# Moving the axis changes of queries, keys and tokens from TensorE to SBUF-to-SBUF DMAs with VectorE block transposes, and projecting in pairs

## The chip, the core and the metric

The kernel runs on one core of a Trainium2 chip. A core has five engines, each with its own in-order instruction stream: TensorE (PE, matrix products, with weight loads PEld that overlap them), VectorE (DVE), ScalarE (ACT), GpSimd (POOL) and SyncE (SP, which here only issues DMAs). They share an SBUF of 128 partitions. Matrix products go to PSUM. Engines wait for one another, and for DMAs, through semaphores. An instruction that waits holds up everything behind it on its engine.

The metric is the time of one execution on the device, in microseconds (us). Before the change it is 772.0 us, the median of three runs (771.88 to 772.14).

## What is computed

The input `x` is 16 sequences ("batches" below) of 512 tokens with 128 features, all float32. One layer adds to `x` an attention branch and a branch of experts, both fed by a layer norm of `x`:

```
xn = layernorm(x)
# attention: 16 heads of 8 features
q, k, v = xn@Wq, xn@Wk, xn@Wv
q = q / |q| ;  k = k / |k|                       # per head
attn = softmax(causal(8.0 * q @ k.T))
a = (attn @ v) @ Wo
# 8 experts, each token goes to its best 2
p = softmax(xn @ Wr.T); top 2, weights scaled to sum 1
f = sum over the 2 experts of w_e * (gelu(xn @ W1[e].T + b1[e]) @ W2[e].T + b2[e])
return x + a + f
```

The products contract over features, so features must lie on the partitions. The layer norm and the per-head norms leave tokens on the partitions. Something has to change the axes for the normalised tokens (`rows` to `xnT`), for the normalised queries (`qkn` to `qT`) and for the normalised keys (`qkn` to `kr`).

## The kernel before

**Stages.** The attention work is a pipeline of 160 hand-ordered stages, ten for each batch (`PER = 10`), stage `t = 10*b + n`. PE, DVE, ACT and SP keep the order in which the program is written (`manual_schedule`, L924); POOL keeps the order given by `on_pool` (L491). A stage computes score products for batch `b` (`scores`, L655: PE fills two `sim` tiles, ACT takes exponentials of them into `ex`), then a step from the list `side`, then the causal mask of the stage before (`mask`, L682, on DVE when `n` is 1, 4, 6 or 9 and the routing steps are over, otherwise on POOL), then the weighted sum of values of two stages before (`weigh`, L701, PE into the one PSUM bank `av`; after every second or third call DVE transposes `av` into `mid`), and last the steps that `at_stage` planned for this stage (`due`, L1082).

**Preparation of a batch.** `prep(b)` (L551) plans, relative to the batch's first stage: four projections (`proj`, L557, one 128x384 product each, copied out of PSUM by ACT) at -18, -17, -14 and -11; squares on POOL (`squares`, -11 to -9); copies of the values into `vaug` on POOL (`values`); sums of squares and three Newton steps for the inverse root on DVE (`sums`, `root_start`, `root_step`, -7 to -5); the scaling `scale` (L607, DVE) at -4; four PE transposes of queries into a PSUM bank with a DVE copy to `qT` (`turn_q`, L616) at -3; the same for keys into `kr` (`turn_k`, L623) at -2; then four DVE products that keep one head of four each, `kT` (`alone`, L630), at -2, -1, 0 and 1. The batch's first `scores` needs `qT` and the first `kT`.

**Tokens.** Batches 0 to 2 are turned before stage 0. The list `side` (L1029) turns one of batches 3 to 15 in a stage (`turn_x`, L274: four PE transposes, one DVE copy to `xnT`), mixed with the router's logits. Routing steps follow on DVE from stage 20. From then on POOL sends each token's row to two places in DRAM (`send`, L509, 128 indirect DMAs, one or two a stage).

**Experts.** After stage 139 the 71 blocks of the experts run (`experts`, L861), each with four DMAs issued by SP (`fetch`, L776) five blocks ahead. The preparation steps of batch 15 are run inside them, one planned stage every five blocks (L876). The stages of batches 14 and 15 follow.

**Queues.** SP issues the 16 loads of `x`, then 48 DMAs that fill the DRAM table `slots` (L970), and then nothing until the experts. Tiles named from the pool `p1` exist once, those from `p2` twice: a writer waits until all readers of the tile's last use are done. `qkn` and `kr` are single, `qkv` and `qT` are double, and two `vaug` tiles are taken in turn.

Of the kernel before, what the change touches and what calls it, by code (L numbers as in the profile page):

```python
# [10 lines left out]
F32 = mybir.dt.float32  # L11
# [6 lines left out]
HEADS = 16  # L18
# [6 lines left out]
def attention_moe_kernel(  # L25
# [31 lines left out]
    GB = 4  # L57
# [27 lines left out]
    wall = const.tile([P, NQKV], F32, name="wall")  # L85
# [62 lines left out]
    xnT = [xnT2[b // 2][:, b % 2] for b in range(B)]  # L148
# [10 lines left out]
    p1 = pool("p1", 1)  # L159
    p2 = pool("p2", 2)  # L160
# [10 lines left out]
    def misc(name):  # L171
        return ps_m.tile([P, 512], F32, tag="misc", name=name)

    def SIM(name):
# [1 line left out]


    vaugs = [
        p1.tile([P, NC, HEADS, VW], F32, tag=f"vaug{n}", name=f"vaug{n}") for n in range(2)
    ]  # L180


# [91 lines left out]
    def turn_x(b, bank, copy):  # L274

        for c in range(NC):
            nc.tensor.transpose(bank[:, ts(c, P)], rows[b][:, c, :D], ident)
        copy(xnT[b], bank)  # L278


    turned = {}

    def logits(b0):

        lt = misc(f"lt{b0}")
# [205 lines left out]
    def on_pool(op, *args, sent=False, **kw):  # L491

        with ExitStack() as order:
            if issued[0] is not None:
                order.enter_context(tc.issue_after(issued[0].ins))
            if not sent:
                for dma in issued[1]:  # L500
                    order.enter_context(tc.issue_after(dma.ins))
            ins = op(*args, **kw)  # L502
        if sent:
            issued[1].append(ins)
        else:
            issued[:] = [ins, []]
        return ins
# [40 lines left out]
    def at_stage(t, step):  # L548
        plan.setdefault(t, []).append(step)

    def prep(b):  # L551

        t0 = PER * b
        s = live[b] = {}
        s["vaug"] = vaugs[b % 2]

        def proj(c, bank=misc):  # L557
            if not c:
                s["qkv"] = p2.tile([P, NC, NQKV], F32, tag="qkv", name=f"qkv{b}")
            pp = bank(f"proj{b}_{c}")  # L560
            nc.tensor.matmul(  # L561
                pp[:, :NQKV], xnT[b][:, ts(c, P)], wall, start=True, stop=True
            )
            nc.scalar.copy(s["qkv"][:, c], pp[:, :NQKV])  # L564

        heads = lambda t: t.rearrange("p c (h d) -> p c h d", d=DH)
# [7 lines left out]
        def values(c):  # L574
            on_pool(
                nc.gpsimd.tensor_copy,
                s["vaug"][:, c : c + 2, :, 0:DH],
                heads(s["qkv"][:, c : c + 2, 2 * D : 3 * D]),
            )

        n = NC * 2 * HEADS

        def sums():
            s["ss"] = sm.tile([P, n], F32, tag="ss", name=f"ss{b}", bufs=1)
            nc.vector.tensor_reduce(
                s["ss"].rearrange("p (c h) -> p c h", c=NC), heads(s["qkn"]), AX.X, ALU.add
            )

        def root_now(meanwhile):

            s["rn"] = sm.tile([P, n], F32, tag="rn", name=f"rn{b}", bufs=1)
            nc.vector.tensor_scalar_max(s["ss"], s["ss"], L2_EPS * L2_EPS)
            nc.scalar.activation(s["ss"], s["ss"], AF.Sqrt)
            meanwhile()
            nc.vector.reciprocal(s["rn"], s["ss"])

        def root_start():

            s["rn"] = sm.tile([P, n], F32, tag="rn", name=f"rn{b}", bufs=1)
            nc.vector.tensor_scalar_max(s["ss"], s["ss"], L2_EPS * L2_EPS)  # L600
            guess(s["rn"], s["ss"])

        def root_step():
            t = sm.tile([P, n], F32, tag="t", name=f"t{b}")
            newton(s["rn"], s["ss"], t, 1)

        def scale():  # L607
            nc.vector.tensor_mul(
                heads(s["qkn"]),
                heads(s["qkv"][:, :, : 2 * D]),  # L610
                s["rn"].rearrange("p (c h) -> p c h", c=NC).unsqueeze(3).to_broadcast(
                    [P, NC, 2 * HEADS, DH]
                ),
            )

        def turn_q():  # L616
            pt = misc(f"qt{b}")
            for c in range(NC):
                nc.tensor.transpose(pt[:, ts(c, P)], s["qkn"][:, c, :D], ident)  # L619
            s["qT"] = p2.tile([P, S], F32, tag="qT", name=f"qT{b}")  # L620
            nc.vector.tensor_copy(s["qT"], pt)

        def turn_k(bank=misc):  # L623
            pt = bank(f"kt{b}")
            for c in range(NC):
                nc.tensor.transpose(pt[:, ts(c, P)], s["qkn"][:, c, D:], ident)  # L626
            s["kr"] = p1.tile([P, S], F32, tag="turned", name=f"kr{b}")
            nc.vector.tensor_copy(s["kr"], pt)

        def alone(r):  # L630

            if not r:
                s["kT"] = p2.tile([P, NG, S], F32, tag="kT", name=f"kT{b}")
            nc.vector.tensor_scalar_mul(s["kT"][:, r], s["kr"], hmask[:, r : r + 1])  # L634

        if not b:
            return SimpleNamespace(
                proj=proj, squares=squares, values=values, sums=sums, root_now=root_now,
                scale=scale, turn_q=turn_q, turn_k=turn_k, alone=alone,
            )  # L640
        times = (-18, -17, -14, -11) if b > 1 else (-11, -11, -10, -9)
        for c, t in enumerate(times):
            at_stage(t0 + t, lambda c=c: proj(c, SIM if t0 + t < 0 and c else misc))
        for t, step in (
            (-11, lambda: squares(0)), (-11, lambda: squares(1)),
            (-10 + (b == 1), lambda: squares(2)), (-9 + (b == 1), lambda: squares(3)),
            (-8, lambda: values(0)),
            (-7, lambda: values(2)), (-7, sums), (-7, root_start), (-7, root_step),
            (-6, root_step), (-5, root_step), (-4, scale), (-3, turn_q), (-2, turn_k),
            (-2, lambda: alone(0)), (-1, lambda: alone(1)), (0, lambda: alone(2)),  # L650
            (b != B - 1, lambda: alone(3)),
        ):
            at_stage(t0 + t, step)

    def scores(b, n):  # L655
# [328 lines left out]
    for b in range(1, 4):  # L984
        stats(b)
    variance, shifts = scales(1, 4, True)
    for c in range(NC):
        zero.proj(c, SIM if c else misc)
        zero.squares(c)
        if c == 1:  # L990
            variance()
            stats(4)
            shifts()
# [1 line left out]
    normalise(1, (ACT,) * NC)  # L995
    stats(5)
    stats(6)
    zero.values(0)
    zero.values(2)
    normalise(3, (POOL,) * NC)  # L1000
    zero.sums()
    zero.root_now(lambda: stats(7))
# [20 lines left out]

    def turn(b):
        turn_x(b, misc(f"xnt{b}"), nc.vector.tensor_copy)

    side = [  # L1029
        lambda step=step, b=b: step(b)  # L1030
        for step, b in (
            (turn, 3), (turn, 4), (turn, 5), (turn, 6), (turn, 7), (logits, 0),
            (turn_logits, 0), (logits, 4), (turn_logits, 4), (turn, 8), (turn, 9),
            (turn, 10), (turn, 11), (logits, 8), (turn_logits, 8), (turn, 12), (turn, 13),
            (turn, 14), (turn, 15), (logits, 12), (turn_logits, 12),
        )
    ]
# [7 lines left out]
    for t, steps in enumerate(feed):  # L1045
        for step in steps:
            at_stage(t, step)

    (places, later) = place()

# [12 lines left out]
    def stage(t, b, n):  # L1063

        due_masks = masks[:]
        del masks[:]
        if b is not None:
            for _ in range(2 if t % PER in (1, 5, 8) else 1):
                if sends:
                    sends.pop(0)()  # L1070
            if (b, n) != (FIRST, 0):
                scores(b, n)
                pending.append((b, n))
        if side:
            side.pop(0)()
# [84 lines left out]
```

## Time and profile before

The profile is of one execution. That execution took 773.95 us, and its span (first to last instruction) is 772.2 us. The median of the timed runs is 772.0 us, so 1.95 us have to be taken off a sum made against the profiled execution.

| part | us from the span's start | PE busy | DVE busy | ACT busy | POOL busy |
|---|---|---|---|---|---|
| whole span | 0 to 772.2 | 731.1 | 516.6 | 464.8 | 485.9 |
| loads, batch 0 prepared | 0 to 20 | 13.5 | 13.4 | 6.7 | 9.6 |
| first stages | 40 to 70 | 29.0 | 21.4 | 21.9 | 21.3 |
| routing | 150 to 200 | 45.5 | 40.9 | 32.8 | 40.5 |
| attention, later batches | 250 to 300 | 50.0 | 40.6 | 39.7 | 43.6 |
| experts | 440 to 660 | 218.5 | 111.1 | 90.6 | 113.9 |

A row says how long an engine executed instructions in that stretch; what a stretch is limited by is the engine that has no idle time left or, where none is full, the chain of waits. The batches' first stages, read from the `sim` products in the timeline of PE, start at 61.4 (batch 1), 95.8 (2), 122.8 (3), 155.3 (4), 188.9 (5), 217.5 (6), 246.1 (7), then every 26.5 us to 405.1 (13). The experts start at 431.6.

### The profile page before, as it was taken

What the parts mean: (1) busy time and instruction counts of PE and PEld (TensorE: products, weight loads), DVE (VectorE), ACT (ScalarE), POOL (GpSimd) and SP (SyncE); (2) the same over time, 40 slices, a digit from 0 to 9 for tenths busy, and PEclk for the clock granted to TensorE, in tenths of its full rate; (3) what the DMA queues carried; (4) which work ended last, traced back from release to release, by engine and by line L of the source; (5) the groups of instructions that cost most, each with busy time, mean ns of one, the idle gap of its engine ahead of it and who ended that gap; (6) DMA issues with size and microseconds to landing.
All of it is one profiled execution on the core that took longest, in us unless ns stands there. A gap on an engine that the chain in (4) does not pass through costs nothing.

```text
span 772.2 us, 17655 instructions
## 1 busy us (share of the span) xinstructions
PE 731.1 (95%) x6478; PEld 450.4 (58%) x6478; DVE 516.6 (67%) x1128; ACT 464.8 (60%) x703; POOL 485.9 (63%) x576
## 2 busy tenths in 40 slices
PE   6899999989999999999999899999999999998994
PEld 2344444334334444444444499989999999996441
DVE  6876678798987887887788445455554445442584
ACT  3767676567777778777878544433444444446771
POOL 4658444388898888888888255554555455556441
PEclk9999999999999999999999999999999999999996
DMA  9940000001101111110110698877777787850596
GB/s 264 326 149 2 1 2 1 1 20 32 33 29 37 37 34 33 36 37 29 38 37 32 194 280 229 229 223 210 235 222 226 222 233 224 233 167 6 187 283 183
DMA packets 91829, 96.48 MB, mean 125 GB/s; under 512 B 10956, under 2 KB 69455, under 8 KB 91744
## 3 DMA queue, kind: packets, MB, share of 16 engines
q1 hardware_dynamic: 82240, 78.01, 35.4%
q0 software_dynamic: 8640, 17.06, 6.5%
q8 instruction: 52, 0.85, 0.4%
q10 hardware_dynamic: 864, 0.28, 0.2%
q14 instruction: 33, 0.27, 0.1%
HBM read 64.34 MB, written 31.88 MB: 125 GB/s over the span
## 4 chain that ended last, share of the span: by engine, by line
PE 80%; DVE 14%; DMA 2%; ACT 1%; issue 1%; POOL 1%; DVEq 0%; POOLq 0%
PE sim L665 17%; PE av L708 17%; PE av L828 16%; PE ph L817 16%; PE proj L561 5%; DMA yt<-results 2%; DVE x L908 2%; PE xgt L796 2%; PE po L752 2%; DVE mid L720 1%; PE qt L619 1%; PE kt L626 1%; DVE st L206 1%; PE idle L959 1%; DVE kT L634 1%
## 5 line engine op out<-in xcount | busy, mean ns | idle before, releaser
L675 ACT ACTIVATE ex<-sim 128x1024 f32<-128x1024 f32 x320 | 310.0, 1022 | 105.4 <-PE sim L665 100.7
L502 POOL DMA_INDIRECT results<-y,to x142 | 139.0, 979 | 138.5 <-DVE y L836 111.8
L820 ACT ACTIVATE gT<-ph,bias 128x256 f32<-128x256 f32 x284 | 111.4, 475 | 158.4 <-PE ph L817 154.0
L665 PE MATMUL sim<-qT,kT 32*128 32x512 f32 (+3 forms) x2048 | 190.1, 463 | 0.7 <-ACT ex L675 0.7
L708 PE MATMUL av<-ex,vaug 128*12 128x512 f32 (+3 forms) x2048 | 171.5, 442 | 16.1 <-DVE mid L720 10.0
L502 POOL TENSOR_SCALAR_AFFINE_SELECT ex<-ex 128x512 f32<-128x512 f32 (+1 forms) x144 | 115.2, 808 | 84.3 <-ACT ex L675 82.6
L502 POOL DMA_INDIRECT slots<-rows,pos x128 | 140.7, 1099 | 28.8 <-issue 25.8
L665 PEld LDWEIGHTS sim<-qT,kT 32*128 32x128 f32 x2048 | 95.7, 185 | 77.8 <-issue 34.0
L828 PE MATMUL av<-xnT,gT 128*128 128x128 f32 x1136 | 138.7, 275 | 1.4 <-ACT gT L820 0.9
L817 PE MATMUL ph<-xgT,xnT 128*128 128x256 f32 x568 | 134.7, 380 | 1.5 <-DVE xgT L798 1.5
L828 PEld LDWEIGHTS av<-xnT,gT 128*128 128x128 f32 x1136 | 132.4, 192 | 2.6 <-issue 1.5
L708 PEld LDWEIGHTS av<-ex,vaug 128*12 128x12 f32 x2048 | 43.0, 92 | 129.3 <-issue 85.5
L817 PEld LDWEIGHTS ph<-xgT,xnT 128*128 128x128 f32 x568 | 102.5, 190 | 13.4 <-DVE xgT L798 1.9
L798 DVE COPY xgT<-xgt 128x256 f32<-128x256 f32 x71 | 30.1, 424 | 68.9 <-PE xgt L796 68.7
L833 DVE TENSOR_TENSOR y<-av,bb 128x256 f32<-128x256 f32 x71 | 30.1, 425 | 67.2 <-PE av L828 67.2
L720 DVE STREAM_TRANSPOSE mid<-av 128x512 f32<-128x512 f32 x64 | 45.5, 711 | 40.6 <-PE av L708 40.4
L561 PE MATMUL proj<-wall,xnT 128*128 128x384 f32 x128 | 58.3, 542 | 5.4 <-DVE xnT L278 2.9
L502 POOL TENSOR_TENSOR qkn<-qkv 128x256 f32<-128x256 f32 x64 | 54.9, 867 | 9.9 <-ACT qkv L564 9.5
L686 DVE TENSOR_TENSOR ex<-ex,causal 128x1024 f32<-128x1024 f32 x40 | 52.0, 1300 | 3.4 <-ACT ex L675 3.4
L634 DVE TENSOR_SCALAR kT<-kr,hmask 128x512 f32<-128x512 f32 x64 | 40.5, 635 | 0.6
L564 ACT COPY qkv<-proj 128x384 f32<-128x384 f32 x64 | 30.9, 482 | 14.1 <-PE proj L561 13.9
L561 PEld LDWEIGHTS proj<-wall,xnT 128*128 128x128 f32 x128 | 19.5, 190 | 32.6 <-issue 16.3
(144 smaller groups left out, 584.8 us busy)
## 6 DMA issues: line engine op xcount, KB each, us to landing
xnT<-in_w1T_dram SPq DMA_DIRECT2D x71, 256.0 KB, 3.5
xnT<-in_w2T_dram SPq DMA_DIRECT2D x71, 256.0 KB
slots<-fill SPq DMA_DIRECT2D x48, 198.0 KB, 5.1
xg<-slots SPq DMA_DIRECT2D x71, 132.0 KB
yt<-results SPq DMA_DIRECT2D x16, 512.0 KB, 5.1
bb<-in_b_dram SPq DMA_DIRECT2D x71, 64.0 KB
x<-in_x_dram SPq DMA_DIRECT2D x16, 256.0 KB, 4.7
out_dram<-x SPq DMA_DIRECT2D x16, 256.0 KB, 5.5
```

The costliest lines, as they stand in the source:

```text
L502: ins = op(*args, **kw)
L561: nc.tensor.matmul(pp[:, :NQKV], xnT[b][:, ts(c, P)], wall, start=True, stop=True)
L564: nc.scalar.copy(s["qkv"][:, c], pp[:, :NQKV])
L634: nc.vector.tensor_scalar_mul(s["kT"][:, r], s["kr"], hmask[:, r : r + 1])
L665: nc.tensor.matmul(halves[g // 2][:, g % 2, col : col + (NC - j) * P], s["kT"][group, r, ts(j, P)], s["qT"][group, j * P :], start=True, s ...
L675: nc.scalar.activation(ex[:, 2 * h : 2 * h + 2], half, AF.Exp, scale=SCALE)
L686: nc.vector.tensor_mul(diag, diag, causal.unsqueeze(1).unsqueeze(1).to_broadcast([P, NG, many, P]),)
L708: nc.tensor.matmul(av[32 * g : 32 * g + VW, j * P :], s["vaug"][:, j, NG * g + r], s[m][:, g, col : col + (NC - j) * P], start=(j == 0), s ...
L720: nc.vector.transpose(s["mid"][:, r], av)
L817: nc.tensor.matmul(ph[:, m], s["w1"][:, ts(m, P)], s["xgT"], start=True, stop=True)
L820: nc.scalar.activation(s["gT"][:, m], ph[:, m], AF.Gelu, bias=bias1[:, i, m : m + 1])
L828: nc.tensor.matmul(py[:, c], s["gT"][:, m, ts(c, P)], s["w2"][:, m], start=(m == 0), stop=(m == NM - 1),)
```

## The change

- Tokens of batches 4 to 15, and queries and keys of batches 2 to 15, no longer pass through PE. A new helper `ferry` issues 16 DMAs on SP for a 128x512 tile. Each moves a block of 32 partitions by 4 chunks by 32 numbers (runs of 128 bytes, 16 KB) to where the block belongs after the turn. One VectorE instruction then transposes inside all 32x32 blocks.
- `carry_x(b)` ferries the tokens of two batches (32 DMAs) and `land_x(b)` transposes them; `carry` ferries queries and keys of one batch (32 DMAs), and `turn_q` and `turn_k` transpose them. All use one single tile, `z`.
- Two projections share a `sim` tile of PSUM, two banks; ACT copies queries and keys out in one instruction and the values straight to `vaug` in another. The POOL copies `values` go. There are three `vaug` tiles; `qkv` loses its third part and becomes single.
- Steps of a batch's preparation move: projections to -14 and -11, squares to -13, -12, -10 and -9, sums to -8, `scale` and `carry` to -5 (`carry` of batch 2 one later).
- The `side` list keeps batch 3 and the logits. Token crossings are issued at stages 2, 4, 8, 10, 12, 14 and landed at 4, 7, 10, 12, 14, 16.

```diff
+    def ferry(to, what):
+        blocks = to.rearrange("p (c t f) -> p c t f", c=NC, f=TB)
+        for f in range(D // TB):
+            for t in range(P // TB):
+                nc.sync.dma_start(
+                    blocks[ts(f, TB), :, t], what[ts(t, TB), :, ts(f, TB)]
+                )
+    crossing = {}
+    def carry_x(b):
+        z = crossing[b] = p1.tile([P, 2, S], F32, tag="z", name=f"zx{b}")
+        for k in range(2):
+            ferry(z[:, k], rows[b + k][:, :, :D])
+    def land_x(b):
+        nc.vector.transpose(
+            xnT2[b // 2].rearrange("p k s -> p (k s)"),
+            crossing.pop(b).rearrange("p k s -> p (k s)"),
+        )
...
-            nc.scalar.copy(s["qkv"][:, c], pp[:, :NQKV])
+            pp = s["pp"] = ps_sim.tile([P, 2, S], F32, tag="sim", name=f"proj{b}_{c}")
+            for k in range(2):
+                nc.tensor.matmul(
+                    pp[:, k, :NQKV], xnT[b][:, ts(c + k, P)], wall, start=True, stop=True
+                )
...
+            if b:
+                nc.scalar.copy(s["qkv"][:, c : c + 2], pp[:, :, : 2 * D])
+            return lambda: nc.scalar.copy(
+                s["vaug"][:, c : c + 2, :, 0:DH], heads(pp[:, :, 2 * D : NQKV])
+            )
...
+        def carry():
+            z = s["z"] = p1.tile([P, 2, S], F32, tag="z", name=f"z{b}")
+            for k in range(2):
+                ferry(z[:, k], s["qkn"][:, :, k * D : (k + 1) * D])
         def turn_q():
+            s["qT"] = p2.tile([P, S], F32, tag="qT", name=f"qT{b}")
+            if "z" in s:
+                nc.vector.transpose(s["qT"], s["z"][:, 0])
+                return
...
         def turn_k(bank=misc):
+            s["kr"] = p1.tile([P, S], F32, tag="turned", name=f"kr{b}")
+            if "z" in s:
+                nc.vector.transpose(s["kr"], s["z"][:, 1])
+                return
...
-        times = (-18, -17, -14, -11) if b > 1 else (-11, -11, -10, -9)
+        if b > 1:
+            twos = ((0, -14), (2, -11))
+            squared = (-13, -12, -10, -9)
+            steps = [
+                (-8, sums), (-8, root_start), (-8, root_step), (-7, root_step),
+                (-6, root_step), (-5, scale), (-5 + (b == 2), carry),
+                (-3 + (b == 2), turn_q), (-2 + (b == 2), turn_k),
+                (-2 + (b == 2), lambda: alone(0)),
+            ]
...
+    crossings = ((4, 2, 4), (6, 4, 7), (8, 8, 10), (10, 10, 12), (12, 12, 14), (14, 14, 16))
+    for b, _, t in crossings:
+        at_stage(t, lambda b=b: land_x(b))
...
+    for b, t, _ in crossings:
+        at_stage(t, lambda b=b: carry_x(b))
```

More of the change, by code (lines that the diff above doesn't have):

```diff
@@ L178, in attention_moe_kernel @@
     vaugs = [
-        p1.tile([P, NC, HEADS, VW], F32, tag=f"vaug{n}", name=f"vaug{n}") for n in range(2)
+        p1.tile([P, NC, HEADS, VW], F32, tag=f"vaug{n}", name=f"vaug{n}") for n in range(3)
     ]
@@ L554, in prep, with proj @@
         s = live[b] = {}
-        s["vaug"] = vaugs[b % 2]
-        def proj(c, bank=misc):
+        s["vaug"] = vaugs[b % 3]
+        heads = lambda t: t.rearrange("p c (h d) -> p c h d", d=DH)
+        def proj(c):
             if not c:
[L559 to L562, printed above, removed]
-            )
-            nc.scalar.copy(s["qkv"][:, c], pp[:, :NQKV])
-        heads = lambda t: t.rearrange("p c (h d) -> p c h d", d=DH)
+                s["qkv"] = p1.tile([P, NC, 2 * D], F32, tag="qkv", name=f"qkv{b}")
+            pp = s["pp"] = ps_sim.tile([P, 2, S], F32, tag="sim", name=f"proj{b}_{c}")
[3 more added lines that the diff above has]
+                )
+                if not b:
+                    nc.scalar.copy(s["qkv"][:, c + k], pp[:, k, : 2 * D])
+            if b:
+                nc.scalar.copy(s["qkv"][:, c : c + 2], pp[:, :, : 2 * D])
+            return lambda: nc.scalar.copy(
+                s["vaug"][:, c : c + 2, :, 0:DH], heads(pp[:, :, 2 * D : NQKV])
+            )
         def squares(c):
@@ L572, in squares @@
             on_pool(nc.gpsimd.tensor_mul, s["qkn"][:, c], qk, qk)
[L574 to L579, printed above, removed]
         n = NC * 2 * HEADS
@@ L619, in turn_q @@
                 nc.tensor.transpose(pt[:, ts(c, P)], s["qkn"][:, c, :D], ident)
-            s["qT"] = p2.tile([P, S], F32, tag="qT", name=f"qT{b}")
             nc.vector.tensor_copy(s["qT"], pt)
         def turn_k(bank=misc):
+            s["kr"] = p1.tile([P, S], F32, tag="turned", name=f"kr{b}")
+            if "z" in s:
+                nc.vector.transpose(s["kr"], s["z"][:, 1])
+                return
             pt = bank(f"kt{b}")
@@ L626, in turn_k @@
                 nc.tensor.transpose(pt[:, ts(c, P)], s["qkn"][:, c, D:], ident)
-            s["kr"] = p1.tile([P, S], F32, tag="turned", name=f"kr{b}")
             nc.vector.tensor_copy(s["kr"], pt)
@@ L637, in prep @@
             return SimpleNamespace(
-                proj=proj, squares=squares, values=values, sums=sums, root_now=root_now,
+                proj=proj, squares=squares, sums=sums, root_now=root_now,
                 scale=scale, turn_q=turn_q, turn_k=turn_k, alone=alone,
             )
-        times = (-18, -17, -14, -11) if b > 1 else (-11, -11, -10, -9)
[L642 to L652, printed above, removed]
+        if b > 1:
[7 more added lines that the diff above has]
+            ]
+        else:
+            twos = ((0, -11), (2, -10))
+            squared = (-11, -11, -9, -9)
+            steps = [
+                (-7, sums), (-7, root_start), (-7, root_step), (-6, root_step),
+                (-5, root_step), (-4, scale), (-3, turn_q), (-2, turn_k),
+                (-2, lambda: alone(0)),
+            ]
+        for c, t in twos:
+            at_stage(t0 + t, lambda c=c: proj(c)())
+        for c, t in enumerate(squared):
+            at_stage(t0 + t, lambda c=c: squares(c))
+        steps += [(-1, lambda: alone(1)), (0, lambda: alone(2))]
+        for t, step in steps + [(b != B - 1, lambda: alone(3))]:
             at_stage(t0 + t, step)
@@ L986, in attention_moe_kernel @@
     variance, shifts = scales(1, 4, True)
+    values = []
     for c in range(NC):
-        zero.proj(c, SIM if c else misc)
+        if c % 2 == 0:
+            values.append(zero.proj(c))
         zero.squares(c)
@@ L997, in attention_moe_kernel @@
     stats(6)
-    zero.values(0)
-    zero.values(2)
+    for step in values:
+        step()
     normalise(3, (POOL,) * NC)
@@ L1022, in attention_moe_kernel @@
     at_stage(1, lambda: zero.alone(3))
[L1026 to L1037, printed above, removed]
+    side = {0: lambda: turn_x(3, misc("xnt3"), nc.vector.tensor_copy)}
+    for n, t in enumerate((1, 8, 13, 18)):
+        side[t] = lambda n=n: logits(GB * n)
+        side[t + 1] = lambda n=n: turn_logits(GB * n)
+    crossings = ((4, 2, 4), (6, 4, 7), (8, 8, 10), (10, 10, 12), (12, 12, 14), (14, 14, 16))
+    for b, _, t in crossings:
+        at_stage(t, lambda b=b: land_x(b))
     variance, first, second, shifts = scales(8, B, False)
@@ L1073, in stage @@
                 pending.append((b, n))
-        if side:
-            side.pop(0)()
+        if t in side:
+            side.pop(t)()
         for args in due_masks:
```

## The prediction, made before the changed kernel ran

> **What bounds the kernel now.** I read the page's busy rows first, then the timelines of PE and DVE in a late batch, then SP's DMA issues. The page says that PE carries the span:
>
> ```profile
> PE 731.1 (95%) x6478; PEld 450.4 (58%) x6478; DVE 516.6 (67%) x1128; ACT 464.8 (60%) x703; POOL 485.9 (63%) x576
> PE 80%; DVE 14%; DMA 2%; ACT 1%; issue 1%; POOL 1%; DVEq 0%; POOLq 0%
> ```
>
> In the timeline of PE around the start of batch 8 (start, duration in us) nothing is idle, and the removed transposes lie on the path:
>
> ```profile
> 266.90 0.66 PE L619 MATMUL qt<-ident,qkn 128*128 128x128 f32 x4
> 267.48 1.14 PE L665 MATMUL sim<-qT,kT 32*128 32x512 f32 x8
> 268.55 1.05 PE L708 MATMUL av<-ex,vaug 128*12 128x384 f32 x16
> 269.54 0.66 PE L626 MATMUL kt<-ident,qkn 128*128 128x128 f32 x4
> 270.12 1.15 PE L665 MATMUL sim<-qT,kT 32*128 32x384 f32 x16
> ...
> 272.60 1.14 PE L665 MATMUL sim<-qT,kT 32*128 32x512 f32 x8
> ```
>
> The timeline of DVE shows the margin: `scale` ends at 266.1, the last input, the first `kT`, at 271.6, and batch 8's first product starts at 272.60, one microsecond later.
>
> ```profile
> 264.87 1.18 DVE L608 TENSOR_TENSOR qkn<-qkv,rn 128x1024 f32<-128x1024 f32 x1
> 267.59 0.69 DVE L621 COPY qT<-qt 128x512 f32<-128x512 f32 x1 [0.41 <-PE qt L619]
> 270.23 0.69 DVE L628 COPY kr<-kt 128x512 f32<-128x512 f32 x1 [1.95 <-PE kt L626]
> 270.96 0.63 DVE L634 TENSOR_SCALAR kT<-kr,hmask 128x512 f32<-128x512 f32 x1
> ```
>
> SP has issued nothing between 45 and 428 us, so its queue is free for the change. What one issue costs is in the answers on `slots` (min/median/max ns) and in SP's timeline (start, total of three):
>
> ```profile
> L971 SPq DMA_DIRECT2D slots<-fill x48: 319/320/850, 14.5 to 44.8; - x48
> 0.82 1.55 SPq L82 DMA_DIRECT2D x<-in_x_dram  x3
> ```
>
> **What is removed.** One set of four PE transposes takes 0.58 us of PE (269.54 to 270.12). Gone are 28 sets of queries and keys and 12 of tokens: 40 x 0.58 = 23.2 us of a PE that is full. The DVE copies (0.69) become block transposes of the same size; the nearest row, L747's 128x512 SBUF transpose, takes 0.70, so DVE neither gains nor loses. POOL loses 30 copies of 0.47; it isn't the bound. ACT's four copies of 0.48 a batch (1.93) become two of 512 columns (0.58, the ACT row of `xnT`) and two of 256 (0.48, the row of `gT`): 2.1. Bounds -0.3 and +0.5 a batch; ACT has 20% idle, which hides it, and would cost 3 us over all batches if it didn't. The projections are the same products; a pair holds one of the three `sim` tiles for about 1.1 us, hidden in the waits below.
>
> **What is added: issue time.** A carry is 32 DMAs on SP, 640 in all. No row shows a 16 KB SBUF-to-SBUF DMA, so I bound it.
> - Issue. The cheapest of SP's 48 fills took 0.32 us, and the closest two starts in the trace are 0.365 apart. Issued back to back with no wait the fills start at 15.204, 15.704, 16.197 and 16.692 (0.49 apart); later neighbours are 0.474 apart; the loads of `x` 0.50 to 0.55. Fills have 128 runs like a ferry. Ends 0.365 and 0.55; I take 0.48.
> - Landing. SP's first load is issued at 0.82 and its first packet starts at 2.10: 1.28 us. The 128-byte packets in the trace take 13 ns, eight for each of 16 engines. With completion I estimate 1.6 us from issue to landing; ends 1.4, and 5.1 (fills and `yt`, which move 198 and 512 KB).
> - One carry: 31 x 0.48 + 1.6 = 16.5 us. Ends 31 x 0.365 + 1.6 = 12.9, and 24.9 if landing took 5.1: the program gives SP's DMAs eight semaphores in turn, so each would wait for the one eight before (5.1 / 8 = 0.64 apart).
>
> **A rule against the row.** The Trainium skill, page "DMA: Bandwidth & Descriptors", section "Issuing engines are not separate DMA queues", says that the sequencer's time to initiate a DMA is usually small beside the DMA itself. By it a carry is its data: 4096 packets x 13 ns / 16 engines = 3.4 us, plus 1.6, is 5.0 us, and the two stages (5.3 us) between carry and turn hide it: the change would save 23 us. By the row it is 16.5 us and nothing hides it. The same page's "Rules for kernel authors" speaks against the change: transfers under 64 KB are mostly overhead. I take the row.
>
> **The token crossings, one chain.** The tile `z` is single, so a carry can start only after the landing of the one before, and a landing sits in DVE's queue, two or three stages after its carry. Behind it in that queue are batch 1's Newton steps, `mid` (PE waits for it to reuse `av`) and `kT`; stalled DVE soon stops PE. SP is also busy with fills until 45.2 us. One round: carry 16.5 + transpose of twice 0.70 + two semaphores, estimated at 0.1 each = 18.1. Six rounds end at 45.2 + 108.6 = 153.8. Batch 2's own carry then lands at 170.3. Before, stage 16 began at 82.0: the work between (14 stages of some 3.3 us, 46 us) fits inside the waits.
>
> **Each later batch.** From a batch's first product to the end of the next batch's `scale` it took 19.9 us in batches 7 to 13 (246.11 to 266.05), 20.4 in 2, 25.4 in 3, 27.0 in 4, 22.3 in 5 and 6. The new order puts one Newton step and one `mid` behind `scale`: minus 2.3. Then the carry: 0.1 + 16.5. Then not DVE (0.69 + 0.65) but POOL sets the end: `qkn` is single, so the next batch's first square, planned for -13, waits for all 32 DMAs, and behind it on POOL are two sends and stage 7's mask, which `weigh` needs before PE comes to the batch's first product. That tail: square 0.87 + two sends of 1.1 + mask 1.1 + `weigh` 0.62 + pair of projections 0.85 + 0.1 = 5.7 (3.5 while there are no sends, batches 2 to 4).
>
> **The clock.** PE now stands for over 10 us in each batch. Here gaps of 1.2 us (before 125.15) and 2.2 us (before 166.71) were followed by stretches at half clock:
>
> ```profile
> 126.00:129.00 3.00, 3.00 (x32) 2.43 (x28) 2.36 (x6) 0.55 (x1) 1.22 (x2) 1.00 0.02 5
> 129.60:133.00 3.40, 3.40 (x38) 1.69 (x32) 1.37 (x3) 1.94 (x2) 1.11 (x2) 0.50 0.00 0
> ```
>
> PEclk is the third number from the end. Page "TensorE: Matmul & The Clock Gate", section "Part 1", makes it a rule: an idle window of 3.4 us brings half clock, a busy one full clock. By the row alone (two losses in 380 us) it costs 3 us; by the rule about 1.7 us a batch, 17 us. I take 1.7, except in batches 3 and 4, whose times have it already.
>
> **The sum.** Batch 2 starts at 170.3 + 3.5 = 173.8 (before 95.8). The next periods: batch 2: 20.4 - 2.3 + 1.7 + 16.6 + 3.5 = 39.9. Batch 3: 25.4 - 2.3 + 16.6 + 3.5 = 43.2. Batch 4: 27.0 - 2.3 + 16.6 + 5.7 = 47.0. Batches 5 and 6: 44.0 each. Batches 7 to 13: 19.9 - 2.3 + 1.7 + 16.6 + 5.7 = 41.6 each, 291.2. The experts start at 683.1 in place of 431.5: +251.6. Inside them batch 15's carry puts 15.4 us of issues before SP's fetches, which are five blocks of 3.7 us ahead and need 3.5 to land, so 15 us are covered: cost 0 to 8, I take 4, less 1.2 of transposes. So 773.95 + 251.6 + 2.8 = 1028.4, less 1.95 against the median: **1026 us**.
>
> **Rivals.**
> - *Short issue* (22%): neighbours 0.365 apart, POOL's tail and the clock hidden. Round 14.5, batch 2 at 146.6, periods 32.6, 37.6, 39.2, 34.5, 34.5 and seven of 32.1: experts at 549.7, time about 893. For it: the 0.32 median; against: neighbours without waits are never that close twice running.
> - *Slow landing* (11%): eight in flight bind, 24.9 a carry, 8.4 x 19 more: about 1186. For it: landings of 5.1; against: those move far more bytes.
> - *Hidden carries, faster* (4%): 772.0 - 23.2 = 749. `scale` would end at 263.8, `kr` must start by 270, so a carry must take 6.2 us: 0.15 us an issue. Above that it decides the other way. For it: SP and the DMA engines idle; against: no SP issue under 0.319.
>
> My forecast has 62%, no change to be told 1%. What a measurement can tell from no change is 0.2%: faster 0.04, same 0.01, slower 0.95. The range, 895 to 1095, takes in 0.365 to 0.55 an issue and most of the short case.
>
> **What will show it.** SP: 640 issues about 0.48 apart in bursts of 15 us. DVE: long waits of `xnT`, `qT` and `kr` on DMAs. POOL's `qkn` on DMAs, PE idle over 10 us before each batch's first product, half clock after it. It is wrong if a burst takes 5 us, or if batch 2 starts before 130.

## The result, and the profile after

The changed kernel takes 1155.83 us (four runs, 1155.33 to 1161.64), beside 772.07 us (771.88 to 774.57) for the kernel before on the same chip. The ratio is **1.4964**, 95% interval 1.4905 to 1.5023. Ratios here are formed from fast executions alone, since a kernel runs some per cent slower in some executions, so a ratio can differ from the quotient of the medians beside it. Sign and mechanism were forecast, but 1155.8 lies 130 us above the forecast and outside its range. The profiled execution has a span of 1159.9 us.

From the profile, first the busy rows, then the chain that ended last, by engine and by line (shares of the span):

```profile
PE 757.6 (65%) x6318; PEld 455.6 (39%) x6318; DVE 493.4 (43%) x1122; ACT 465.4 (40%) x705; POOL 456.5 (39%) x546
PE 35%; SPq 34%; DVE 12%; DMA 8%; issue 5%; POOL 4%; ACT 2%; POOLq 0%; ACTq 0%; DVEq 0%
```

PE lost 160 instructions and yet is busy longer (the granted clock is 0.824 over the span, 0.986 before; see below), and it is no longer the bound: 95% of the span has become 65%. A third of the path now runs through SPq, SP's issuing, which was not on the path at all.

The view of tile `z` gives the durations of the issues (min/median/max, ns), and the time from issue to landing (us):

```profile
L286 SPq DMA_DIRECT2D z<-qkn x448: 585/599/1915, 189.0 to 945.9; - x150
DMA to landing us min/median/max: 1.8/1.8/4.0
```

No issue was shorter than 0.585 us; the cheapest fills had taken 0.319. A landing takes 1.8 us, near the 1.6 assumed. So the data is quick and the issuing is slow. SP's own waits for earlier crossings to land (us in total, times, longest) are short beside the 640 issues:

```profile
SPq L286 <- DMA z<-qkn: 13.4, 24, 0.6
SPq L286 <- DMA zx<-rows: 6.8, 12, 0.6
```

The waits (who waited for what: total us, times, longest):

```profile
POOL qkn L526 <- DMA z<-qkn: 306.6, 13, 55.3
...
PE av L756 <- POOL ex L526: 247.2, 15, 20.9
...
DVE qT L650 <- DMA z<-qkn: 124.7, 13, 10.9
...
DVE kr L660 <- DMA z<-qkn: 110.9, 12, 9.6
DVE xnT L299 <- DMA zx<-rows: 107.6, 6, 23.3
```

These are the four waits named ahead of the run: tokens, queries and keys on DVE, and the square on POOL. PE hangs behind POOL, not behind DVE, except for the token crossings at the start.

One late batch shows the chain. The timelines of SP, DVE, POOL and PE ahead of batch 10's first product follow, each with start, duration, and in brackets the idle time before and its releaser. SP:

```profile
581.05 21.48 SPq L286 DMA_DIRECT2D z<-qkn  x32
```

DVE:

```profile
579.76 1.22 DVE L633 TENSOR_TENSOR qkn<-qkv,rn 128x1024 f32<-128x1024 f32 x1
...
593.77 0.71 DVE L650 STREAM_TRANSPOSE qT<-z 128x512 f32<-128x512 f32 x1 [9.83 <-DMA z<-qkn]
604.06 0.71 DVE L660 STREAM_TRANSPOSE kr<-z 128x512 f32<-128x512 f32 x1 [9.58 <-DMA z<-qkn]
604.81 0.51 DVE L671 TENSOR_SCALAR kT<-kr,hmask 128x512 f32<-128x512 f32 x1
```

POOL:

```profile
604.09 0.61 POOL L526 TENSOR_TENSOR qkn<-qkv 128x256 f32<-128x256 f32 x1 [21.47 <-DMA z<-qkn]
604.86 1.01 POOL L526 DMA_INDIRECT slots<-rows,pos  x1 [0.16 <-issue]
606.17 0.97 POOL L526 DMA_INDIRECT slots<-rows,pos  x1 [0.30 <-issue]
607.16 1.11 POOL L526 TENSOR_SCALAR_AFFINE_SELECT ex<-ex 128x1024 f32<-128x1024 f32 x1
```

PE:

```profile
608.32 1.05 PE L756 MATMUL av<-ex,vaug 128*12 128x256 f32 x8 [19.84 <-POOL ex L526]
609.30 2.93 PE L589 MATMUL proj<-wall,xnT 128*128 128x384 f32 x4
612.16 1.24 PE L713 MATMUL sim<-qT,kT 32*128 32x512 f32 x4
```

`scale` ends at 581.0 and SP starts at once. The last block is there at 604.0: the carry is 23 us. `kT` is ready at 605.3, but PE is still in the stage before, because its `weigh` needs a mask that POOL made only at 608.3, behind the square and two sends. `weigh` (1.05 instead of 0.62) and the pair of projections (2.93 instead of 1.56) then run at half clock: the granted clock from 608.30 to 612.20 is 0.50.

| from a batch's first product (batch 9, us) | predicted | measured |
|---|---|---|
| to the end of the next batch's `scale` | 17.6 + 1.7 for the clock | 17.2 |
| carry, to the last landing | 16.6 | 23.0 |
| tail to the next first product | 5.7 | 8.2 |
| period | 41.6 | 48.3 |

### The profile page after: what moved, and what is told of

The parts are those of the page before. It is cut to its first block, busy times and chain, and to the rows that moved or that the text cites. A ratio compares the mean times of both kernels' runs of the same rounds, so it can differ in the third digit from the quotient of the medians.

```text
span 1159.9 us, 18213 instructions
## 1 busy us (share of the span) xinstructions
PE 757.6 (65%) x6318; PEld 455.6 (39%) x6318; DVE 493.4 (43%) x1122; ACT 465.4 (40%) x705; POOL 456.5 (39%) x546
## 4 chain that ended last, share of the span: by engine, by line
PE 35%; SPq 34%; DVE 12%; DMA 8%; issue 5%; POOL 4%; ACT 2%; POOLq 0%; ACTq 0%; DVEq 0%
SPq L286 33%; PE av L876 10%; PE ph L865 10%; PE av L756 5%; PE sim L713 4%; PE proj L589 3%; POOL ex L526 2%; DMA slots<-fill 2%; DMA z<-qkn 2%; ACT ex L723 2%; DVE x L956 1%; DMA yt<-results 1%; PE xgt L844 1%; DVE ss L610 1%; DVE ex L734 1%
## 5 line engine op out<-in xcount | busy, mean ns | idle before, releaser
L756 PE MATMUL av<-ex,vaug 128*12 128x512 f32 (+3 forms) x2048 | 187.1, 468 | 306.9 <-POOL ex L526 247.2
L713 PE MATMUL sim<-qT,kT 32*128 32x512 f32 (+3 forms) x2048 | 207.0, 490 | 1.0 <-ACT ex L723 0.7
L526 POOL TENSOR_TENSOR qkn<-qkv 128x256 f32<-128x256 f32 x64 | 41.0, 641 | 351.4 <-DMA z<-qkn 306.6
L526 POOL DMA_INDIRECT slots<-rows,pos x128 | 131.6, 1028 | 28.9 <-issue 27.1
L713 PEld LDWEIGHTS sim<-qT,kT 32*128 32x128 f32 x2048 | 105.1, 194 | 95.2 <-issue 41.0
L595 ACT COPY qkv<-proj 128x512 f32<-128x512 f32 x30 | 17.6, 586 | 293.4 <-PE proj L589 277.9
L589 PE MATMUL proj<-wall,xnT 128*128 128x384 f32 x128 | 67.4, 661 | 1.6 <-ACT qkv L593 0.9
L650 DVE STREAM_TRANSPOSE qT<-z 128x512 f32<-128x512 f32 x14 | 10.0, 711 | 124.7 <-DMA z<-qkn 124.7
L660 DVE STREAM_TRANSPOSE kr<-z 128x512 f32<-128x512 f32 x14 | 9.9, 708 | 110.9 <-DMA z<-qkn 110.9
L299 DVE STREAM_TRANSPOSE xnT<-zx 128x1024 f32<-128x1024 f32 x6 | 7.5, 1246 | 107.6 <-DMA zx<-rows 107.6
```

The costliest lines, as they stand in the source:

```text
L589: nc.tensor.matmul(pp[:, k, :NQKV], xnT[b][:, ts(c + k, P)], wall, start=True, stop=True)
L713: nc.tensor.matmul(halves[g // 2][:, g % 2, col : col + (NC - j) * P], s["kT"][group, r, ts(j, P)], s["qT"][group, j * P :], start=True, s ...
L756: nc.tensor.matmul(av[32 * g : 32 * g + VW, j * P :], s["vaug"][:, j, NG * g + r], s[m][:, g, col : col + (NC - j) * P], start=(j == 0), s ...
```

## The experiments

All ratios are against the kernel before on the same chip, whose medians were 772 to 774 and, for two groups of runs, 779.5 and 782.1; so ratios are compared, not times. "Batch 2 starts" and "period" are read from each profile as above: the first `sim` product of a batch, and the time from it to the next batch's.

### What makes an issue on SP dear?

The kernel before, with 88 DMAs of 16 to 64 KB that nobody needs issued by SP behind the fills, in six forms.

> The kernel before, with 88 extra SBUF writes by DMA behind SP's fills, in six groups, whose data nobody reads: (1) 16 DMAs of 32 partitions x 8 chunks x 32 numbers, (2) 16 of the ferry's own form 32x4x32, (3) 16 of 32x128 in one run of 512 bytes, (4) 16 of 128x32, (5) 16 of 32x4x32 with DRAM as the source, (6) 8 of 128x4x32. All but (5) go from SBUF to SBUF. In the changed kernel ferries start 0.644 us apart, where the prediction had 0.48. Theory A, the cost goes with the number of runs that a DMA names on both sides: (2), (4), (5) 0.64, (3) clearly less (0.45), (1) 0.9 to 1.2, (6) over 1.5. Theory B, it is the three-level form of the pattern, whatever the number of runs: (1), (2), (5), (6) all 0.60 to 0.68, (3) and (4) 0.45 to 0.50. Theory C, it is SBUF on both sides: (1) to (4) and (6) 0.64, (5) 0.45 to 0.50. Time as before, 772, plus at most 10 for tiles that come free later.

One execution, 774.12 us beside 772.99 (771.85 to 774.09): the probe cost the kernel nothing that can be told. Its DMAs in SP's timeline (the total of a row runs from its first start to its last end):

```profile
44.18 11.64 SPq L978 DMA_DIRECT2D xnT<-x  x16
55.86 33.88 SPq L978 DMA_DIRECT2D sel<-x  x48
89.78 7.71 SPq L978 DMA_DIRECT2D sel<-in_w1T_dram  x16
97.53 6.25 SPq L978 DMA_DIRECT2D sel<-x  x8
```

The medians between neighbouring starts, read from the trace:

| form | from, to | runs | between starts, us | duration, us |
|---|---|---|---|---|
| 32x4x32, as `ferry` | SBUF, SBUF | 128 of 128 bytes | 0.644 | 0.599 |
| 32x128 | SBUF, SBUF | 32 of 512 bytes | 0.634 | 0.589 |
| 128x32 | SBUF, SBUF | 128 of 128 bytes | 0.644 | 0.599 |
| 32x8x32 (32 KB) | SBUF, SBUF | 256 of 128 bytes | 0.654 | 0.609 |
| 128x4x32 (64 KB) | SBUF, SBUF | 512 of 128 bytes | 0.683 | 0.638 |
| 32x4x32 | DRAM, SBUF | 128 of 128 bytes | 0.474 | 0.430 |

Neither the number of runs nor their length nor the bytes decide: from 32 runs to 512 the spacing rises by 0.05. Taking the data out of DRAM instead of SBUF lowers it by 0.17. So 0.474, the spacing of the closer fills in the trace of before, holds for a DMA with one end in DRAM and not for these. In each group with both ends in SBUF one issue also took 1.3 to 1.7 us. In the kernel after, 12 of the 640 issues took over 1 us; with or without one of them, the 32 issues of a carry take 20.6 to 21.9 us. Why two ends in SBUF are dearer, the probe doesn't show.

### Half as many DMAs for the same bytes

```diff
-        blocks = to.rearrange("p (c t f) -> p c t f", c=NC, f=TB)
+        blocks = to.rearrange("p (c t f) -> p c t f", t=P // TB, f=TB)
...
-            z = s["z"] = p1.tile([P, 2, S], F32, tag="z", name=f"z{b}")
-            for k in range(2):
-                ferry(z[:, k], s["qkn"][:, :, k * D : (k + 1) * D])
+            z = p1.tile([P, 2, S], F32, tag="z", name=f"z{b}")
+            ferry(
+                z.rearrange("p k s -> p (k s)"),
+                s["qkn"].rearrange("p c (k d) -> p (c k) d", d=D),
+            )
...
```

The same for the tokens: a carry is 16 DMAs of 32 KB. `turn_q` and `turn_k` then pick their blocks out of `z`.

> The changed kernel with queries and keys (or the tokens of two batches) in one ferry: 16 DMAs of 32x8x32 in place of 32 of 32x4x32, the same bytes and runs. If an issue has a fixed price of 0.644 us, a carry falls from 21.8 to 15 x 0.644 + 1.8 = 11.5 us; 19 carries x 10.3 us lie on the chain, so about 1156 - 195 = 960 us, less if PE stays at full clock. If the price goes with the runs in a DMA, 16 issues cost 1.1 to 1.3 us each and the time stays at 1120 to 1160 us.

956.98 us, ratio 1.238 (1.2336 to 1.2425). The `z` row shows half the issues at nearly the same duration each:

```profile
L286 SPq DMA_DIRECT2D z<-qkn x224: 585/610/1801, 129.6 to 741.1; - x112
```

Batch 2 starts at 148.1 instead of 217.1 and late periods are about 38 instead of 48.5. The bytes are the same, so the price is one for each issue, as expected (960). This takes back half of the loss and shows at the same time that even 16 issues, some 11 us, aren't hidden.

### One crossing at a time

Queries and keys alone: tokens are turned by PE again, with the `side` list of before and no `carry_x`.

> The changed kernel with the tokens turned by TensorE again, in the order of the kernel before; queries and keys still cross by DMA. My theory, a chain of seven carries ahead of batch 2 and then one carry in each batch: batch 2 starts near 108 us in place of 217, the periods of 48 to 50 us and the experts stay, time 1040 to 1055 us. Rival, that SP's traffic or DVE as such sets the pace of all stages: the periods shorten too, and the time falls below 1000 us.

1050.9 us, ratio 1.3596 (1.3536 to 1.3655). Batch 2 starts at 112.9, periods stay at 46 to 52: the token crossings only delay the start, as one chain.

Tokens alone: no `carry`, queries and keys are turned by PE, and squares move with them.

```diff
-            squared = (-13, -12, -10, -9)
+            squared = (-11, -11, -10, -9)
...
-                (-6, root_step), (-5, scale), (-5 + (b == 2), carry),
+                (-6, root_step), (-5, scale),
```

> The changed kernel with queries and keys turned by TensorE again (no carry in a batch; squares at -11, -11, -10, -9, since queries and keys are read until -2); the tokens still cross by DMA. My theory: batch 2 starts near 195 to 205 us (six carries), after that the periods are those of before (26 to 33 us) and the experts need no more than before: 870 to 890 us. Rival, that the pairs of projections or the moved steps slow the batches by themselves: periods stay over 35 us, time over 980 us.

904.27 us, ratio 1.1699 (1.1646 to 1.1751): above what was expected. Batch 2 starts at 197.3, as it should, but late periods are 30.3 and not 26.5. Something in the change besides the crossings costs nearly 4 us a batch.

### No crossing at all: what the rest of the change costs

Both edits together: what stays are the pairs, ACT's copies, three `vaug`, the single `qkv`, and the preparation steps at their new places.

> Neither tokens nor queries and keys cross by DMA: the changed kernel's pairs of projections, values by ScalarE, three vaug tiles and earlier sums, with all axes turned by TensorE. With the tokens alone crossing, the batches took 30.3 us in place of 26.5; its trace shows that the sums, moved to -8, now stand ahead of the transpose oT in VectorE's queue and that TensorE waits 2.3 us for oT and then runs a window at half clock. Theory A, it is this order: 772 + 11 to 13 batches x 3.8 = 810 to 825 us, with the wait of po for oT in each batch. Theory B, that loss came from the crossings: 765 to 775 us.

809.7 us (five executions, 803.16 to 815.28), ratio 1.031 (1.0284 to 1.0336), with periods of 30.5 in the profiled execution, which took 814.77. In the timelines of PE and DVE around one of them:

```profile
296.96 0.62 PE L756 MATMUL av<-ex,vaug 128*12 128x256 f32 x8
299.76 1.65 PE L800 MATMUL po<-wo_sb,oT 128*128 128x128 f32 x8 [2.18 <-DVE oT L795]
```

```profile
294.67 1.21 DVE L610 TENSOR_REDUCE ss<-qkn 128x128 f32<-128x1024 f32 x1
295.92 0.89 DVE L625 TENSOR_SCALAR ss<-ss 128x128 f32<-128x128 f32 x1
...
299.01 0.70 DVE L795 STREAM_TRANSPOSE oT<-o 128x512 f32<-128x512 f32 x1
```

With the sums moved from -7 to -8 they and the first Newton step stand ahead of `oT` in DVE's queue, 4.3 us of work, and PE waits 2.2 us for `oT`. This applies to after too, where that wait is 1.2 us in batch 9.

Two more runs take this apart. First, `finish(b)` is planned ahead of `prep(b + 2)`, so that `oT` stands ahead of the sums:

> As the run with pairs alone, but finish(b) is planned ahead of prep(b + 2), so that oT stands ahead of the sums in VectorE's queue. By theory A the wait of po for oT goes and the batches take 26.5 us again: 765 to 775 us. If a pair's hold on a sim tile is what costs, 800 us or more.

796.95 us, ratio 1.0211 (1.0182 to 1.0239), periods 28.7: a third of the loss by the ratios, where all of it was expected. That wait for `oT` is gone from the later batches, but PE now waits for `mid` (21.1 us in all, 10.0 in before) and for DVE's mask (6.8). Second, the run with pairs alone (`finish` in its old place) with DVE's steps at their old stages and `qkv` double again:

```diff
-                s["qkv"] = p1.tile([P, NC, 2 * D], F32, tag="qkv", name=f"qkv{b}")
+                s["qkv"] = p2.tile([P, NC, 2 * D], F32, tag="qkv", name=f"qkv{b}")
...
-                (-8, sums), (-8, root_start), (-8, root_step), (-7, root_step),
-                (-6, root_step), (-5, scale),
-                (-3 + (b == 2), turn_q), (-2 + (b == 2), turn_k),
-                (-2 + (b == 2), lambda: alone(0)),
+                (-7, sums), (-7, root_start), (-7, root_step), (-6, root_step),
+                (-5, root_step), (-4, scale), (-3, turn_q), (-2, turn_k),
+                (-2, lambda: alone(0)),
```

> Pairs of projections, values by ScalarE and three vaug tiles, all axes turned by TensorE, and VectorE's steps at the places of the kernel before (sums at -7, scale at -4), qkv double again. If the 25 to 38 us that the runs with pairs lost come from the sums and Newton steps that moved ahead of masks and of mid in VectorE's queue, this one is at the time of before: ratio 0.995 to 1.005. If pairs holding a sim tile cost by themselves, ratio 1.015 or more.

780.2 us (16 executions) beside 782.06, ratio **0.996** (0.994 to 0.998). So the pairs, the joint copies and the values straight to `vaug` cost nothing, and may bring 0.4%. It is the only version of the change here that is not slower than the kernel before. The 3.5% between it and the run with pairs alone are the moved steps, together with the single `qkv`, which this run doesn't separate from them.

### POOL's tail

After, with the squares two stages later, so that none stands in POOL's queue ahead of stage 9's mask:

```diff
-            squared = (-13, -12, -10, -9)
+            squared = (-11, -11, -10, -9)
```

> The changed kernel with the squares at -11, -11, -10 and -9 in place of -13, -12, -10, -9, so that stage 7's and 8's masks are ahead of the square that waits for the carry on GpSimd. The prediction's step: after the carry lands, GpSimd's square, two sends, a mask, the weighted sum and a pair of projections set the start of the batch, 8.4 us as measured. If so, only kr and the first kT stay behind the landing (1.5 us), about 6 us less in each of 12 batches: 1156 - 72 = 1085 us, at most 30 us to either side. If GpSimd's tail is not what sets it: 1140 to 1160 us.

1118.59 us, ratio 1.4345 (1.4312 to 1.4377), just above the 1055 to 1115 expected. PE's timeline ahead of a batch's first product, and DVE's before it:

```profile
608.09 1.56 PE L589 MATMUL proj<-wall,xnT 128*128 128x384 f32 x4
623.88 2.09 PE L713 MATMUL sim<-qT,kT 32*128 32x512 f32 x8 [14.24 <-DVE kT L671]
```

```profile
622.25 0.71 DVE L660 STREAM_TRANSPOSE kr<-z 128x512 f32<-128x512 f32 x1 [9.59 <-DMA z<-qkn]
623.00 0.74 DVE L671 TENSOR_SCALAR kT<-kr,hmask 128x512 f32<-128x512 f32 x1
```

The tail is now the turn and the mask of `kT` alone: 1.6 us from landing to first product instead of 8.2, and late periods are about 44. `weigh` and the projections are done before the wait. So POOL's queue did set the end, as predicted. Of the 6.6 us only some 4.4 show in the period: `scale` ends 19.4 us after the batch's first product instead of 17.2. The half clock, which fell on the tail, now falls on the batch's first stages (2.09 for the eight products in place of 1.14).

### The clock

If the wait costs PE its clock, products that nobody needs, issued in the wait, should keep it:

```diff
+        if b is not None and 0 < b < FIRST and n == PER - 1:
+            for _ in range(33):
+                nc.tensor.matmul(
+                    misc("idle")[:, :NQKV], wo_sb, wall, start=True, stop=True
+                )
         if b is None or len(pending) > LAG:
             weigh(*pending.pop(0))
```

> The changed kernel with 33 products of 384 columns, whose results nobody reads, ahead of stage 9's weighted sum in batches 1 to 13: 33 x 0.56 = 18.5 us of TensorE work in a wait of some 20 us. It tells what the half clock after the wait costs. If the clock stays full, the tail behind the carry falls from 8.4 to 6 us and the first stages get up to 2 us shorter: 12 x 2 to 4 us, 1110 to 1135 us. If the clock costs nothing that matters: 1150 to 1160 us. If the added products themselves run at half clock they overshoot the wait and the time rises above 1165 us.

1314.78 us, ratio 1.6784 (1.6702 to 1.6865): the filling was too long. In PE's timeline it takes 32 us in a wait of 20:

```profile
632.07 31.98 PE L1127 MATMUL idle<-wall,wo_sb 128*128 128x384 f32 x66
663.97 0.62 PE L756 MATMUL av<-ex,vaug 128*12 128x256 f32 x8
664.52 1.56 PE L589 MATMUL proj<-wall,xnT 128*128 128x384 f32 x4
```

Each product is two passes (66 for 33) and takes 0.97 us instead of the 0.56 expected, at full clock (1.00 from 632 to 664). The projections, of the same size, take 1.56 for two: with the filler, PE's weight loads wait for the product before (0.67 us each time). But `weigh` and the pair took 2.0 us to the first product, not 3.8 as in after. With 19 products:

> As the run with 33 added products, which took 0.97 us each in place of 0.56 (two passes a product) and overshot the wait by some 11 us a batch, but with 19: 18.4 us of TensorE work in a wait of 20 us. With TensorE at full clock the weighted sum and the pair ahead of a batch's first product took 2.0 us in that run, against 3.5 to 3.9 in the changed kernel. So half clock there costs 1.5 to 1.9 us a batch, with the first stages 2 to 3.5: 12 x 2 to 3 us less, 1120 to 1132 us, if the wait is filled well; 1145 to 1160 us if the clock is not what matters.

1167.02 us, ratio 1.5076 (1.5014 to 1.5139): no gain where 25 to 35 us were expected. In batches 1 and 3 the last mask ahead of `weigh` had ended 7.7 and 4.8 us before the filler did (at 214.2 and 221.9, at 320.3 and 325.1); batch 4 starts 13 us later than in after. From there to batch 13 the run wins back 9.

Two periods show why it isn't more. The first pair of rows is batch 8 in after and here, the second pair batch 12 in after and here (busy time and count of PE, PEld, DVE, ACT, POOL; then the granted clock, DMA share and GB/s):

```profile
515.40:563.80 48.40, 26.80 (x273) 11.67 (x272) 18.65 (x32) 21.12 (x24) 21.15 (x23) 0.79 0.13 30
523.20:571.50 48.30, 44.37 (x315) 17.02 (x314) 20.94 (x33) 21.11 (x24) 21.52 (x24) 0.96 0.13 30
```

```profile
709.10:757.90 48.80, 27.63 (x273) 11.82 (x272) 19.62 (x33) 21.11 (x24) 21.10 (x23) 0.78 0.13 30
715.60:761.80 46.20, 42.57 (x311) 16.73 (x310) 18.99 (x33) 21.11 (x24) 20.39 (x23) 1.00 0.13 30
```

In batch 8 the tail did get shorter by 1.8 us, but `scale` came 18.8 us after the batch's first product instead of 17.2, so the period didn't move. The carry starts when DVE is done with `scale`, and DVE's instructions had become longer: `o` 1.13 us instead of 0.69, `ss` (L625) 1.07 instead of 0.23, `t` (L211) 0.81 instead of 0.30. The largest of these differences, in DVE's and POOL's timelines here, then in DVE's of after in batch 9:

```profile
532.90 1.07 DVE L625 TENSOR_SCALAR ss<-ss 128x128 f32<-128x128 f32 x1
532.77 1.11 POOL L526 TENSOR_SCALAR_AFFINE_SELECT ex<-ex 128x1024 f32<-128x1024 f32 x1
```

```profile
573.08 0.23 DVE L625 TENSOR_SCALAR ss<-ss 128x128 f32<-128x128 f32 x1
```

Here `ss` ran beside a mask of POOL and ended with it; in after the same mask ended (572.9) before `ss` began. Why `ss` is slower beside the mask the traces don't show. In batch 12 DVE and POOL are in step again as in after's batch 9: `ss` takes 0.23, `scale` comes at 17.1 in both, and the period is 46.2 instead of 48.3. So in this one pair of periods with DVE's steps equal the half clock costs 2.1 us; in the others a later `scale` took all or part of it away.

### A carry early enough to be hidden?

Merged carries, tokens by PE, `oT` ahead of the sums, and the preparation earlier: projections by two stages, sums, `scale` and `carry` by three (`scale` and `carry` at -8), squares at -13 and -12, each two stages less for batch 2. So the 11 us of issues would lie beside five stages of products.

> Queries and keys cross by DMA in merged ferries of 16 DMAs (carry 15 x 0.644 + 1.8 = 11.5 us) that are issued at -8 and taken at -3 and -2, five stages later (13 us); projections, squares and sums three stages or two earlier; tokens turned by TensorE; oT ahead of the sums. If issue time against the distance to its reader is the whole cost, carries are hidden and TensorE is spared 1.17 us a batch: 755 to 768 us. If the block transposes or SP's traffic slow the stages by themselves, or squares wait for carries on GpSimd, over 780 us.

852.98 us, ratio 1.0926 (1.0898 to 1.0954): far better than after, and still a miss. In the later batches `scale` ends 13.6 to 14.2 us after the batch's first product, although its stage is the third of ten in a period of 32 to 33 us; the next squares still wait for the carry (50.7 us in all, 6.9 at most), `qT` waits up to 3.7 us, and PE waits for POOL's masks (30.0 in all). Which of these is the last bound was not separated. A second `qkn`, which would free the squares, was not tried. Nor were issues shared among several engines' queues, or a way through DRAM.

## Why the prediction was wrong, and where it was right

The ratios give the parts, in units of 772 us. Pairs with moved steps: 0.031, 24 us (30 by the medians). Queries and keys on top, with the squares at their new places (1.3596 less 1.031): 254 us. Tokens on top of that (1.4964 less 1.3596): 106 us. Tokens without queries and keys (1.1699 less 1.031) cost 107 us, so the two crossings add.

**The failed step: the price of an issue.** The prediction took "0.48", between "ends 0.365 and 0.55", from loads and fills, and said itself that no row showed a DMA inside SBUF. It measured 0.644, outside both ends; the probe shows that two ends in SBUF make the difference to 0.474. With 1.8 to land, a carry is 23.0 us and not 16.5. The upper end of the range was built on 0.55, so the range missed as well.

The span (1159.9) exceeds the sum on the profiled span (772.2 + 251.6 + 2.8 = 1026.6) by 133 us, and 120 of these lie ahead of the experts. Batch 2 starts at 217.1, 43 late. Of this 35 are the six rounds of tokens, which took 23.9 us each and not 18.1; the first and the last of the six transposes in DVE's timeline:

```profile
68.23 1.25 DVE L299 STREAM_TRANSPOSE xnT<-zx 128x1024 f32<-128x1024 f32 x1 [23.28 <-DMA zx<-rows]
187.72 1.25 DVE L299 STREAM_TRANSPOSE xnT<-zx 128x1024 f32<-128x1024 f32 x1 [19.11 <-DMA zx<-rows]
```

The rest is batch 2's own carry and tail. The twelve periods after it are 6.4 too long each, as much as the carry, but partly by luck: in batch 9 the tail was 2.5 longer than forecast and `scale` 2.1 earlier, and these two errors cancel.

**A reading in the sum.** Batch 4 of the kernel before was said to start at 155.3. That is the last stage of batch 3; batch 4's first product, of 512 columns, starts at 157.79. So its "27.0" to `scale` is 24.5, and the sum should have been 2.5 us lower, a little further from the result.

**The rival "slow landing": near in number, not in cause.** It named 1186 us and 0.64 us between issues, both nearer to what was measured than the forecast. But it rested on landings of 5.1 us that hold the ninth issue back. Landings took 1.8, and SP waited for them only 36 times in 640 issues, 20 us in all.

**The rule against the row.** The Trainium skill ("DMA: Bandwidth & Descriptors", "Issuing engines are not separate DMA queues") would have made a carry its data, 5.0 us with landing by the prediction's estimate; SP was busy issuing for 21.5. Preferring the row was right. Taking it unchanged for another pair of memories was the mistake.

**The token chain: right, but for the price of a round.** DVE waits 107.6 us for tokens to land in the single `z`; without the token crossings batch 2 starts at 112.9.

**What sets the end: right.** POOL's square, two sends, mask: the first `weigh` waits for POOL, and moving the squares took the tail away. Its size was 8.2 instead of 5.7. POOL's share came as forecast (4.2 us for square, sends and mask). PE's did not: `weigh` and the pair took 3.8 instead of 1.5. About 0.6 of it is a slip, since "pair of projections 0.85" is the time of one projection (the row in before is 0.91 for one), and the other 1.8 is half clock, as the run with 33 products shows (2.0 at full clock).

**The clock: right in size, not in place.** The long wait does bring half clock, in the tail (about 2 us) more than in the first stages, where the 1.7 had been put. In the one pair of periods with DVE's steps equal, full clock was worth 2.1 us; over the whole run the filler gained nothing.

**DVE order: missed.** "Minus 2.3" counted what was put behind `scale` and not what the moved sums were put ahead of. With TensorE turning everything, the moved steps and the single `qkv` cost 3.5%. In after this is small beside the carries: `scale` came at 17.2, even before the 19.3 forecast.

**The experts: too small.** "0 to 8, I take 4": from the first to the last `ph` product they take 283.0 us in place of 267.7. Timelines of SP and PE:

```profile
919.53 0.33 SPq L838 DMA_DIRECT2D bb<-in_b_dram  x1
924.80 21.74 SPq L286 DMA_DIRECT2D z<-qkn  x32
947.19 0.39 SPq L831 DMA_DIRECT2D xg<-slots  x1
```

```profile
949.52 0.66 PE L844 MATMUL xgt<-ident,xg 128*128 128x128 f32 x2 [13.92 <-DMA xg<-slots]
```

SP waited 5 us for `scale` to end and only then issued for 21.7, so 27.7 us passed between fetches. PE ran on for 16 us after the last fetch (to 935.6), near the 15 estimated, and then stood for 13.9. That SP would first wait for `scale` was not in the estimate.

## What to carry to other kernels

Price a DMA's issue by a row with the same two memories at its ends; if the trace has none, widen the range upwards, and multiply before anything else: 640 issues at 0.6 us are 400 us of one queue. An axis change moved off TensorE can pay only if the whole transfer, issues included, fits between its input and its use; here it replaced 0.58 us of products by 10 us of queue, and no run made it fit. And a step that is moved in an in-order queue must be priced by what then stands behind it.

## What was not expected of the hardware

- An SP issue with both ends in SBUF takes 0.60 us (0.644 between starts), with one end in DRAM 0.43 (0.474), for the same blocks; 32 to 256 runs make no more than 0.02 us of difference, 512 runs 0.05.
- A short VectorE instruction beside one of GpSimd's can take several times as long: 0.23 us alone, 1.07 us beside a mask of 1.11 us. So a change of TensorE's clock came back through VectorE's and GpSimd's order.
- With the same filler, raising TensorE's clock shortened one period by 2.1 us and left another as it was (0.96 instead of 0.79).
- A filler product with 384 columns takes 0.97 us at full clock where two projections of that size take 1.56, because its weight loads wait for the product before.
